# A two-step graph layer with guessed thresholds: gathers one by one, the laws' end later, two pieces of the end moved

## The chip, the cores and the metric

The kernel runs on one core of a Trainium2 chip. The engines are TensorE (PE, with PEld for its weight loads), VectorE (DVE), ScalarE (ACT), GpSimd (POOL) and SyncE (SP, which here only issues DMAs). Each engine takes its instructions in the order of its own queue, and waits for others through semaphores. The metric is the device time of one execution in microseconds (us), as a median of several runs; less is better. A profiled execution, a run of its own, gives the trace.

## What is computed

The inputs are x (3327 rows of 256) and an adjacency matrix adj (3327 x 3327, some 0.12% of it not zero, and its diagonal). The reference, cut to what matters:

```python
def _top_p_attention(X, W1, W2, W3):
    logits = (X @ W1.T @ W2.T) @ (X @ W3.T).T
    probs = softmax(logits, axis=-1)
    idx = argsort(-probs)
    sp = take_along_axis(probs, idx); cs = cumsum(sp)
    keep_sorted = cs - sp < 0.9            # the largest, up to a mass of 0.9
    A = probs * mask                       # mask: keep_sorted at its places
    return A / maximum(A.sum(-1), 1e-12)

h = maximum(_layernorm(x), 0.0)
R = (adj + eye) / row sums
Z, Xf, Xa = 0, h, h
for n in range(2):
    A = _top_p_attention(Xa, W1, W2, W3)
    Xf = R @ Xf
    Xa = A @ Xa
    Z = Z + Xf @ U1[n].T + Xa @ U2[n].T
out = x + layernorm(h + Z) * ln_g + ln_b
```

## The kernel before

The 3327 rows make 26 tiles of 128 (NT), the last of 127 rows. Both steps run over the tiles, as a pipeline that is written out by hand: in turn i of a step, tile i's threshold is settled, tile i + 1 is measured, tile i + 2 gets its logits, and the sums of tile i - 1 run on PE. The adjacency is so sparse that R @ X is done by gathering: for each row tile, and each of the 128 places within a column block, there is a list of the blocks that hold anything there; four of the list and one for what overflows are fetched by index, and the tile's own block is added (KT = 6).

For each tile and step:

- `weights` makes the exponentials e of one tile's logits (128 x 3328, PE and ACT).
- `measured` finds a threshold by guessing. `guessed` takes the row's sum Z and the row's "law" (mean, variance and what follows from them) to a first guess; then whole passes over e on ACT (L631, some 3.07 us each) count and sum what lies above. In the second step (`measured_twice`) there are three passes: two at the first guess, then one at a second guess that L682 to L686 compute; POOL makes small terms: L674 and L675 behind the first guess, L687 to L689 behind the second, L694 to L709 behind the third pass; ACT's L711 and DVE's L714 end it.
- `settle` on DVE: w (L728, e below the guess), 20 MAX8 over w (L733), six rounds of MAX8 and replace (L740, L742), the exact threshold (L747 to L752), and e masked by it in place (L762; in tiles 0 and 25 in two parts, L759, the first 1024 columns of 3328).
- `Sums` on PE: `turn` transposes four 128 x 128 blocks of e into PSUM (L811) and ACT copies them to SBUF (L813, eT); `sum` multiplies (L825) into one accumulator pa, of which there is one buffer. `turn` runs two groups ahead of `sum`. The transposes have two PSUM buffers.
- `gathered` (first step) and `refetch` (second step) fetch for R @ X: one DMA by SP for the adjacency blocks, and five gathers issued by POOL (L903, one instruction each) into xg, which has two buffers. `spread` multiplies them (L911) into one accumulator pr; DVE takes it out in L1086.
- `finish` in the second step, cut in pieces by `yield`: DVE takes the sum out of pa (L935), row statistics (L457, L458), POOL's L464, L465, L943, ACT's scaling (L950), POOL's L951 and L952, and the store.

`laws` makes the law of tiles 3 to 25 of the second step, after all of the first step is known. Eight pieces on PE and DVE (L556 to L562), then one end on POOL: a power of 0.5 (L567, a `pow` on 128 x 23) and nine small operations (L569 to L574). Tiles 0 to 2 have their own small laws.

The order is made by strings. Each turn has seven slots (PARTS); in a slot, each letter takes one piece of one generator: m and n are the measuring of tile i + 1 and of the turn before, d and c the settling, s `spread`, w and q the logits, g the gathers, l the laws, f `finish`. Between the slots PE's sums run. What is left of a generator at the end of a turn is run out in the order of a last string. PE, ACT and DVE then keep the order of the text; POOL keeps it from the second step on. A value is waited for where it is used, and everything behind that instruction on its engine waits too.

Before, one g issues all five gathers of a tile; turn -1 issues tile 0's in a slot and tile 1's at its end, behind the laws' end, and turn i issues those of tile i + 2. When all is done, `proof` tests whether every guess was good enough; if not, a slow search (`search_graph_layer`) computes all again.

Of the kernel before, what the change touches and what calls it, by code (L numbers as in the profile page):

```python
# [9 lines left out]
F32 = mybir.dt.float32  # L10
# [3 lines left out]
AF = mybir.ActivationFunctionType  # L14
ALU = mybir.AluOpType
# [3 lines left out]
P = 128  # L19
N = 3327  # L20
D = 256
DA = 64
NT = (N + P - 1) // P
# [297 lines left out]
LNY = 0.25 * math.log(0.72)  # L321

SQG, SQK = ((c[0], c[1] / (2 * c[0]), c[2] - c[1] ** 2 / (4 * c[0])) for c in (PG, PK))
# [15 lines left out]
KT = DIRECT + 2  # L339
# [5 lines left out]
def guess_graph_layer(ctx, tc, x, adj, w1t, w2t, w3t, u1t, u2t, ln_g, ln_b, out, flag):  # L345
    nc = tc.nc

    const = ctx.enter_context(tc.tile_pool(name="const", bufs=1))
    nodes = ctx.enter_context(tc.tile_pool(name="nodes", bufs=1))
    scan = ctx.enter_context(tc.tile_pool(name="scan", bufs=1))  # L350
    adjp = ctx.enter_context(tc.tile_pool(name="adjp", bufs=3))
# [9 lines left out]
    V, G, S, PE = nc.vector, nc.gpsimd, nc.scalar, nc.tensor  # L361

    rows_of = lambda t: min(P, N - t * P)
    valid = lambda t: 0 <= t < NT
# [41 lines left out]
    half = const.tile([P, 4], F32, tag="half", name="half")  # L406
    for k, c in enumerate((-0.5, 0.5, -1.0, -0.5)):
        G.memset(half[:, k : k + 1], c)
    halves = const.tile([P, NT], F32, tag="halves", name="halves")
    G.memset(halves, 0.5)  # L410
    law = const.tile([P, 7, NT], F32, tag="law", name="law")
    one = const.tile([P, 7], F32, tag="one", name="one")
    for k, c in enumerate((1.0, -1.0, 5.0e-4, SQG[1], SQK[1], math.log(10.0), LNY)):
        G.memset(one[:, k : k + 1], c)
    of_s = const.tile([P, 4], F32, tag="of_s", name="of_s")
    for k, c in enumerate((SQG[0], SQG[2], -SQK[0], -SQK[2])):
# [24 lines left out]
    bx = dram.tile([P, NT, D + 1], F32, tag="bx", name="bx")  # L441
    vx = dram.tile([P, NT, D], F32, tag="vx", name="vx")
# [4 lines left out]
    bb = const.tile([P, TOPK + 1], F32, tag="bb", name="bb")  # L447
# [100 lines left out]
    def laws(ts):  # L548

        at = lambda k, a, b: law[:, k, a:b]  # L550
        few_of = [ts[h::2][n : n + 3] for n in range(0, len(ts), 3) for h in range(2)]
        for few in filter(len, few_of):
            pq = ps_t.tile([P, 4, P], F32, tag="pt", name="pq")
            pm = pq.rearrange("p a b -> p (a b)")[:, : 3 * (2 * DA + 2)].rearrange("p (t n) -> p t n", t=3)
            for k, t in enumerate(few):
                PE.matmul(pm[:, k, :], query_of(t), qm[query_at(t), 1, :], start=True, stop=True)  # L556
            wide = scan.tile([P, NP], F32, tag="w", name="wide")
            mq = wide[:, : 3 * (2 * DA + 2)].rearrange("p (t n) -> p t n", t=3)
            V.tensor_copy(mq[:, : len(few)], pm[:, : len(few)])
            V.tensor_copy(law[:, 2, few[0] : few[-1] + 1 : 2], mq[:, : len(few), DA])  # L560
            for k, t in enumerate(few):
                V.scalar_tensor_tensor(mq[:, k, : DA + 1], mq[:, k, : DA + 1], 1.0, mq[:, k, DA + 1 :],  # L562
                                       ALU.mult, ALU.mult, accum_out=at(1, t, t + 1))
            yield
        a, b = ts[0], ts[-1] + 1
        s, var, m = (at(k, a, b) for k in range(3))
        G.tensor_tensor(s, var, halves[:, a:b], ALU.pow)  # L567
        for k, c in ((3, SQG[0]), (4, SQG[2]), (5, -SQK[0]), (6, -SQK[2])):
            G.tensor_scalar(at(k, a, b), s, c, 1.0e-4, ALU.mult, ALU.add)  # L569
        G.tensor_tensor(at(4, a, b), at(4, a, b), var, ALU.add)  # L570
        G.tensor_tensor(at(4, a, b), at(4, a, b), m, ALU.add)
        G.tensor_scalar(m, m, 0.25, LNY - 0.25 * math.log(0.1 / N), ALU.mult, ALU.add)
        G.tensor_scalar(var, var, 0.125, None, ALU.mult)
        G.tensor_tensor(var, var, m, ALU.add)  # L574
# [51 lines left out]
    def con(k):  # L626
        return one[:, k : k + 1]
# [247 lines left out]
    def gathered(t):  # L875
        oh = ohs.pop(t)
        ls, n = lists[:, t, :], LIST - DIRECT
        po = ps_t.tile([P, 4, P], F32, tag="pt", name="po")
        PE.matmul(po[:, 0, : n + 1], oh, ls[:, DIRECT:], start=True, stop=True)
        lo = small.tile([P, n], F32, tag="lo", name="lo", bufs=2)  # L880
        S.copy(lo, po[:, 0, :n])
        nth = small.tile([P, 1], F32, tag="nth", name="nth")
        S.activation(nth, po[:, 0, n : n + 1], AF.Identity, scale=-1.0, bias=part)
        yield
        of = small.tile([P, LIST], F32, tag="of", name="of", bufs=2)
        V.scalar_tensor_tensor(of[:, :n], place[:, :n], nth, lo, ALU.is_equal, ALU.mult, accum_out=nth)
        G.tensor_scalar(index[:, t, DIRECT:], nth, -1.0, float(NONE), ALU.mult, ALU.add)
        ac = adjp.tile([P, KT, P], F32, tag="ac", name="ac", bufs=2)
        nc.sync.dma_start(ac[:, KT - 1, :], adj[t, :, t, :])
        acs[t] = ac  # L890
        G.tensor_tensor(ac[:, KT - 1, :], ac[:, KT - 1, :], ident, ALU.add)
        rows = adj.rearrange("t p j r -> (t p j) r")
        for k in range(KT - 1):
            G.indirect_dma_start(out=ac[:, k, :], out_offset=None, in_=rows,  # L894
                                 in_offset=bass.IndirectOffsetOnAxis(ap=index[:, t, k : k + 1], axis=0),
                                 element_offset=t * P * NT * P)
        xgs[t] = fetched(bx, t, D + 1)

    def fetched(table, t, w):
        xg = adjp.tile([P, KT - 1, D + 1], F32, tag="xg", name="xg", bufs=2)  # L900
        rows = table.rearrange("p j d -> (p j) d")
        for k in range(KT - 1):
            G.indirect_dma_start(out=xg[:, k, :w], out_offset=None, in_=rows,  # L903
                                 in_offset=bass.IndirectOffsetOnAxis(ap=index[:, t, k : k + 1], axis=0))
        return xg


    def diffuse(ac, xg, own, w):
# [55 lines left out]
    live, ohs, acs, xgs, done, early = {}, {}, {}, {}, [], {}  # L964
    none = iter(())

    def run(work, n=99):
        for _ in range(n):
            next(work, None)
# [33 lines left out]
    for q in range(HALF + 5):  # L1003
        if 0 <= q - 3 < HALF:
            k, pk = q - 3, made.pop(q - 3)
# [17 lines left out]
        if 0 <= q - 2 < HALF:  # L1023
            k, pt = q - 2, turned.pop(q - 2)
# [10 lines left out]
        if 0 <= q - 1 < HALF:  # L1035
            k, rn = q - 1, scaled.pop(q - 1)
            pt = ps_t.tile([P, 4, P], F32, tag="pt", name="pt")
            for h in range(2):
                t = 2 * k + h
# [4 lines left out]
        if 0 <= q - 4 < HALF and 2 * (q - 4) in COUNTED:  # L1044
            k = q - 4
# [46 lines left out]
    def refetch(t):  # L1092
        acs[t] = adjp.tile([P, KT, P], F32, tag="ac", name="ac", bufs=2)
        nc.sync.dma_start(acs[t].rearrange("p k r -> p (k r)"), cx[t])
        xgs[t] = fetched(vx, t, D)
        yield

# [1 line left out]


    PLAN = (("mdsssa", "mcdsssa", "edawwp", "msda", "mpdea", "gdwwq", "emgq"),
            ("llcmss", "lnms", "lwwnfd", "lcmdsssg", "fmswqdf", "llmdf", "lmwfd"))

    LAST = {NT - 1: ("cfss", "cn", "ndd", "sss", "fddddsf", "f", "f"), NT: ("cf", "", "", "", "ff", "fv", "f"),
            NT + 1: ("fv", "f", "", "", "f", "f", "f")}
    LATE = (1, 4)
    trace, begin = nc.cur_bb.bb.instructions, len(nc.cur_bb.bb.instructions)
    work = dict(m=none, d=none, f=none)  # L1110
    later = {}
    ordered = []
    for step in range(2):
        sums = Sums(step, live, xw if step else x0, AHEAD[step])

        for i in range(-1, NT + 2):
# [4 lines left out]
            if step == 1 and i == -1:  # L1121
# [6 lines left out]
                c=work["d"],  # L1128
                d=settle(step, i, live[step, i]) if valid(i) else none,
                m=measured(step, live[step, i + 1]) if valid(i + 1) else none,  # L1130
                s=spread(step, i - 2 + 2 * step) if valid(i - 2 + 2 * step) else none,
# [1 line left out]
                e=first_end(i - 2) if step == 0 and valid(i - 2) else none,  # L1133
                a=itertools.islice(lister, 9 if i else 3) if step == 0 else none,
                p=packed(i + 1) if step == 0 and i >= 0 and valid(i + 1) else none,
                g=none if not valid(i + 2 * step) else refetch(i + 2) if step else gathered(i),
                b=none, q=none, v=proof() if step and i == NT else work.get("v", none),
                l=laws(range(3, NT)) if step and i == -1 else none,
            )
            if i >= 0 and valid(i + 3):  # L1140
                later[step, i + 3] = weights(step, i + 3, live)
# [9 lines left out]
                work["w"] = begun[2]  # L1151
            if step == 0 and i < 1:
                work["b"] = itertools.islice(product, MADE if i else NT)
            if step == 1 and i == -1:
                work["g"] = itertools.chain(refetch(0), refetch(1))
            for k in range(PARTS):
                g = PARTS * (i - 1) + k - LATE[step]
                summing = valid(g // PARTS)
                if summing and step:
                    sums.turn(g, min(i, NT - 1))  # L1160
                for c in "bb" + (LAST.get(i, PLAN[1]) if step else PLAN[0])[k]:
                    next(work[c], None)
                if summing and not step:
                    sums.turn(g, min(i, NT - 1))
                if summing:
                    ended = sums.sum(g)
                    if ended and step == 0:
                        live["r", ended[0]] = ended[1]
                    elif ended:
                        work["f"] = finish(ended[0], live.pop(("f", ended[0])), *ended[1])  # L1170
            if step == 1 and i == -1:
                run(work["m"])
            if step == 0 and i == -1:
                G.memset(es[2][:, N:NP], 0.0)
            for c in "lcnwqsepgb" if step else "cmwqsepgb":
                run(work[c])
            if step == 0 and i == NT:
                moments(1, gsum)
# [52 lines left out]
```

## Time and profile before

| | |
|---|---|
| three timed runs | 1426.26, 1431.23, 1432.77 us; median 1431.23 |
| profiled execution | 1383.37 us, its span 1381.4 us |
| busy: PE, DVE, ACT, POOL | 1271.7, 1207.6, 1109.1, 1022.8 us |
| first step ends, second begins | about 740 us |
| ACT pass L631 | 106 of 3.07 us |
| DVE L728 and L762, one | 3.83 and 3.84 us |
| POOL gather of the second step, L903 | 130 of 1.0 us |
| last operation on a tile ends, end of the trace | 1372.2 us, 1381.4 us |

The page lists groups of instructions by line; "out<-in" are the names of the program. The timeline lists instructions by start (us from the span's start), length, engine and line; in brackets stands how long the engine had been idle before, and what released it. In the windows the busy time of each engine in a stretch is given, with the number of its instructions.

### The profile page before, as it was taken

Reading aid. Unit: us, or ns where it says so; the run is one execution under the profiler, and the core shown is the slowest. Engines: PE = TensorE matmul, PEld = TensorE weight load, DVE = VectorE, ACT = ScalarE, POOL = GpSimd, SP = SyncE. Lnnn points to the kernel's source line nnn. Section 1 sums busy time; section 2 is a strip of 40 time slices with the busy share of each in tenths; the row PEclk is TensorE's granted clock in tenths of the full one; section 3 lists DMA queues with packets and bytes.
Section 4 is the critical chain, followed back from the end, with each engine's and each line's share of the span. In section 5 each row is a group of like instructions: output and inputs, shape, how many; then the busy total and the mean of one; then the engine's idle time right before and its main releaser. Section 6 shows DMA issues by size and latency. Waiting matters only on the chain.

```text
span 1381.4 us, 22149 instructions
## 1 busy us (share of the span) xinstructions
PE 1271.7 (92%) x6495; PEld 977.1 (71%) x6495; DVE 1207.6 (87%) x3595; ACT 1109.1 (80%) x2449; POOL 1022.8 (74%) x1374
## 2 busy tenths in 40 slices
PE   6898999999999999999997389999999999999885
PEld 5545777777877778787775267777776777777674
DVE  6878999999999999999944689999999999999992
ACT  5467888879888888888735689999999999999931
POOL 6225888888888888888843868888888888888832
PEclk9999999999999999999998589999999999999998
DMA  8884453545445453545331211212222221212100
GB/s 293 261 271 125 128 148 109 152 119 152 128 135 141 122 154 106 156 118 149 85 98 50 69 54 55 84 58 81 71 67 82 58 88 54 89 58 81 58 8 22
DMA packets 91202, 149.77 MB, mean 108 GB/s; under 512 B 15265, under 2 KB 58656, under 8 KB 91072
## 3 DMA queue, kind: packets, MB, share of 16 engines
q1 hardware_dynamic: 73616, 105.37, 24.4%
q0 software_dynamic: 16640, 42.69, 11.9%
q8 instruction: 54, 0.88, 0.3%
q14 instruction: 76, 0.62, 0.1%
q10 hardware_dynamic: 816, 0.20, 0.1%
HBM read 120.93 MB, written 27.28 MB: 107 GB/s over the span
## 4 chain that ended last, share of the span: by engine, by line
DVE 40%; PE 24%; ACT 17%; POOL 9%; DMA 4%; issue 4%; SPq 0%; POOLq 0%; DVEq 0%; ACTq 0%
ACT ja L631 11%; PE pa L825 9%; DVE e L762 9%; PE pl L598 5%; DVE cand L733 4%; DVE w L728 4%; DVE fm L847 4%; DVE bb L740 3%; DVE cand L742 3%; PE pt L811 3%; PE pz L988 3%; POOL xg L903 3%; POOL ac L894 2%; DVE x L762 2%; DMA at<-in_adj 2%
## 5 line engine op out<-in xcount | busy, mean ns | idle before, releaser
L825 PE MATMUL pa<-xw,eT 128*128 128x256 f32 x1352 | 330.8, 386 | 6.6 <-DVE s L935 6.5
L631 ACT ACTIVATE ja<-e,g 128x3328 uint8<-128x3328 f32 x106 | 325.8, 3074 | 0.1
L825 PE MATMUL pa<-x,eT 128*128 128x256 f32 x1352 | 323.1, 380 | 0.0
L825 PEld LDWEIGHTS pa<-xw,eT 128*128 128x128 f32 x1352 | 249.4, 191 | 67.9 <-issue 27.1
L825 PEld LDWEIGHTS pa<-x,eT 128*128 128x128 f32 x1352 | 243.7, 191 | 25.8
L733 DVE MAX8 cand<-w 128x8 f32<-128x168 f32 (+1 forms) x1040 | 251.5, 318 | 0.0
L813 ACT COPY eT<-pt 128x512 f32<-128x512 f32 (+1 forms) x364 | 201.9, 556 | 59.3 <-PE pt L811 58.8
L894 POOL DMA_INDIRECT ac<-in_adj,index x130 | 189.7, 1459 | 44.3 <-issue 30.5
L811 PE MATMUL pt<-ident,e 128*128 128x128 f32 x1144 | 180.1, 278 | 43.9 <-DVE e L762 21.9
L811 PEld LDWEIGHTS pt<-ident,e 128*128 128x128 f32 x1144 | 140.5, 144 | 90.2 <-issue 43.3
L903 POOL DMA_INDIRECT xg<-bx,index x130 | 158.0, 1216 | 39.2 <-issue 30.5
L728 DVE SCALAR_TENSOR_TENSOR w<-e,g 128x3328 f32<-128x3328 f32 x44 | 168.5, 3830 | 0.7
L903 POOL DMA_INDIRECT xg<-vx,index x130 | 130.9, 1007 | 45.6 <-issue 33.0
L762 DVE SCALAR_TENSOR_TENSOR e<-e,rec 128x3328 f32<-128x3328 f32 x40 | 153.6, 3840 | 0.6
L911 PE MATMUL pr<-xg,ac 128*128 128x257 f32 (+1 forms) x520 | 139.4, 392 | 11.3 <-DVE s L1086 11.1
L602 ACT ACTIVATE e<-pl 128x832 f32<-128x832 f32 x132 | 112.8, 859 | 30.2 <-PE pl L598 30.1
L911 PEld LDWEIGHTS pr<-xg,ac 128*128 128x128 f32 x520 | 94.0, 195 | 25.0 <-DVE s L1086 11.3
L740 DVE MAX8 bb<-cand 128x8 f32<-128x160 f32 x286 | 92.9, 325 | 6.4
L598 PE MATMUL pl<-after,qT 64*128 64x416 f32 x416 | 96.7, 559 | 0.6 <-ACT qT L527 0.6
L765 POOL TENSOR_TENSOR cum<-dr,bb 128x48 f32<-128x48 f32 x26 | 84.8, 3261 | 15.5 <-DVE rec L752 15.4
L951 POOL TENSOR_TENSOR s<-s,gam 128x256 f32<-128x256 f32 x25 | 92.6, 3703 | 3.2 <-ACT s L950 3.2
L598 PE MATMUL pl<-both,qT 64*128 64x416 f32 x416 | 90.1, 536 | 0.8 <-DVE both L1006 0.8
(257 smaller groups left out, 2200.0 us busy)
## 6 DMA issues: line engine op xcount, KB each, us to landing
at<-in_adj SPq DMA_DIRECT2D x102, 256.0 KB, 3.2
cx<-ac SPq DMA_DIRECT2D x26, 384.0 KB, 2.8
ac<-cx SPq DMA_DIRECT2D x26, 384.0 KB, 3.1
wide<-in_adj SPq DMA_DIRECT2D x10, 832.0 KB, 6.4
e<-in_adj SPq DMA_DIRECT2D x8, 832.0 KB, 5.1
bx<-e SPq DMA_DIRECT2D x26, 128.5 KB, 2.8
own<-bx SPq DMA_DIRECT2D x26, 128.5 KB, 3.2
x<-in_x SPq DMA_DIRECT2D x13, 256.0 KB, 5.4
```

The source lines that it names most:

```text
L598: PE.matmul(pl[:, a, :wd], qT[p, :], keys_of(step, a).rearrange("p a b -> p (a b)")[:, c : c + wd], start=True, stop=True)
L631: S.activation(ja, e, f, bias=guess, scale=sign, accum_out=total)
L728: V.scalar_tensor_tensor(w, e, col(16), e, ALU.is_lt, ALU.mult, accum_out=d2)
L733: V.max(cand[:, 8 * s : 8 * s + 8], w[:, s * SEG : min(NP, (s + 1) * SEG)])
L740: V.max(b8, cand)
L762: V.scalar_tensor_tensor(e, e, at(1), e, ALU.is_ge, ALU.mult, accum_out=ra)
L811: PE.transpose(pt[:, j, :], e[:, (j0 + j) * P : (j0 + j + 1) * P], ident)
L813: S.copy(eT[:, :w, :], pt[:, :w, :])
L825: PE.matmul(self.pa, eT[:, c - 4 * k, :], self.xa[:, j, :], start=c == 0, stop=c == NT - 1)
L894: G.indirect_dma_start(out=ac[:, k, :], out_offset=None, in_=rows, in_offset=bass.IndirectOffsetOnAxis(ap=index[:, t, k : k + 1], axis=0), ...
L903: G.indirect_dma_start(out=xg[:, k, :w], out_offset=None, in_=rows, in_offset=bass.IndirectOffsetOnAxis(ap=index[:, t, k : k + 1], axis=0))
L911: PE.matmul(pr[:, :w], ac[:, k, :], own if k == KT - 1 else xg[:, k, :w], start=k == 0, stop=k == KT - 1)
```

## The change

The five gathers of a tile become five pieces, and one generator `fetching` runs through all tiles in order. Strings for the first turns (OPEN) place them: in turn -1 five, one, and one at its end; in turn 0 three, one, and one at its end; in turns 1 to 3 five and one; from turn 4 on five in one slot as before. The laws' end moves from the end of turn -1 to the end of turn 0, and its power becomes Ln and Exp on ACT. In turn 25 (NT - 1), the `finish` piece that takes the third last sum (tile 23) out of pa stands before the twenty MAX8 and not between them, and in the turns 25 and 26 ACT's L950 of that tile stands some copies later.

```diff
-    halves = const.tile([P, NT], F32, tag="halves", name="halves")
-    G.memset(halves, 0.5)
-    one = const.tile([P, 7], F32, tag="one", name="one")
-    for k, c in enumerate((1.0, -1.0, 5.0e-4, SQG[1], SQK[1], math.log(10.0), LNY)):
+    one = const.tile([P, 8], F32, tag="one", name="one")
+    for k, c in enumerate((1.0, -1.0, 5.0e-4, SQG[1], SQK[1], math.log(10.0), LNY, 1.0e-12)):
...
-        G.tensor_tensor(s, var, halves[:, a:b], ALU.pow)
+        S.activation(s, var, AF.Ln, bias=con(7))
+        S.activation(s, s, AF.Exp, scale=0.5)
...
-        xgs[t] = fetched(bx, t, D + 1)
+        run(fetched(bx, t, D + 1))
 
     def fetched(table, t, w):
-        xg = adjp.tile([P, KT - 1, D + 1], F32, tag="xg", name="xg", bufs=2)
+        xgs[t] = xg = adjp.tile([P, KT - 1, D + 1], F32, tag="xg", name="xg", bufs=2)
         rows = table.rearrange("p j d -> (p j) d")
         for k in range(KT - 1):
             G.indirect_dma_start(out=xg[:, k, :w], out_offset=None, in_=rows,
                                  in_offset=bass.IndirectOffsetOnAxis(ap=index[:, t, k : k + 1], axis=0))
-        return xg
+            yield
...
-        xgs[t] = fetched(vx, t, D)
-        yield
+        yield from fetched(vx, t, D)
...
-            ("llcmss", "lnms", "lwwnfd", "lcmdsssg", "fmswqdf", "llmdf", "lmwfd"))
+            ("llcmss", "lnms", "lwwnfd", "lcmdsssggggg", "fmswqdf", "llmdf", "lmwfd"))
 
-    LAST = {NT - 1: ("cfss", "cn", "ndd", "sss", "fddddsf", "f", "f"), NT: ("cf", "", "", "", "ff", "fv", "f"),
+    LAST = {NT - 1: ("cfss", "cn", "nd", "sss", "fdddddsf", "f", ""), NT: ("c", "", "", "ff", "ff", "fv", "f"),
             NT + 1: ("fv", "f", "", "", "f", "f", "f")}
+    OPEN = {-1: ("llcmss", "lnms", "lwwnfd", "lcmdsssggggg", "fmgswqdf", "llmdf", "lmwfdm"),
+            0: ("cmssggg", "nms", "wwnfd", "cmdsss", "fmgswqdf", "mdf", "mwfd"),
+            1: ("cmss", "nms", "wwnfd", "cmdsssggggg", "fmswqdf", "mgdf", "mwfd")}
+    OPEN[2] = OPEN[3] = OPEN[1]
+    fetching = itertools.chain(*(refetch(t) for t in range(NT)))
...
-                g=none if not valid(i + 2 * step) else refetch(i + 2) if step else gathered(i),
+                g=fetching if step else gathered(i) if valid(i) else none,
...
-                l=laws(range(3, NT)) if step and i == -1 else none,
+                l=laws(range(3, NT)) if step and i == -1 else work["l"] if step and i == 0 else none,
...
-            if step == 1 and i == -1:
-                work["g"] = itertools.chain(refetch(0), refetch(1))
...
-                for c in "bb" + (LAST.get(i, PLAN[1]) if step else PLAN[0])[k]:
+                for c in "bb" + ({**OPEN, **LAST}.get(i, PLAN[1]) if step else PLAN[0])[k]:
...
-            for c in "lcnwqsepgb" if step else "cmwqsepgb":
+            if step and i < 1:
+                next(fetching)
+            for c in ("lcnwqsepb" if i > -1 else "cnwqsepb") if step else "cmwqsepgb":
```

## What I expected before the run

> **What bounds the kernel now.** I read the windows first, because two of the three edits touch single places and only a stage table shows what a place is worth. Columns: length, busy time of PE, PEld, DVE, ACT, POOL, the granted TensorE clock, DMA share, GB/s.
>
> ```profile
> 400.00:600.00 200.00, 198.84 (x1060) 158.02 (x1060) 190.56 (x579) 168.38 (x418) 164.35 (x193) 1.00 0.46 130
> ...
> 760.00:780.00 20.00, 8.10 (x22) 4.35 (x22) 12.61 (x40) 12.81 (x25) 15.92 (x27) 0.59 0.22 61
> 780.00:800.00 20.00, 7.30 (x28) 4.49 (x25) 14.89 (x40) 14.59 (x28) 17.12 (x21) 0.59 0.24 70
> ...
> 1000.00:1200.00 200.00, 188.81 (x969) 146.25 (x968) 185.31 (x520) 188.53 (x379) 170.38 (x225) 1.00 0.24 72
> ...
> 1340.00:1382.00 42.00, 24.93 (x132) 20.94 (x130) 13.80 (x42) 6.44 (x13) 9.72 (x17) 0.89 0.06 18
> ```
>
> The first step (to about 740 us) is PE's, 99% busy; the change hardly touches it. In the second step's steady part ACT, PE and DVE are all at 93 to 94%. Between them lies the opening, where PE works 8 of 20 us and POOL is the busiest, and after it the end, where PE works 25 of 42. There the waits are. The timeline of the opening gives the first pair: ACT waits for POOL, then DVE for POOL and ACT for DVE.
>
> ```profile
> 763.61 4.04 POOL L567 TENSOR_TENSOR law<-law,halves 128x23 f32<-128x23 f32 x1
> ...
> 771.00 1.12 POOL L903 DMA_INDIRECT xg<-vx,index  x1 [0.49 <-issue]
> ...
> 777.21 0.33 POOL L674 TENSOR_SCALAR g<-g,ms 128x1 f32<-128x1 f32 x1
> ...
> 777.57 0.29 ACT L685 ACTIVATE g<-g 128x1 f32<-128x1 f32 x1 [4.24 <-POOL g L674]
> ...
> 784.17 0.27 POOL L687 TENSOR_SCALAR g<-g 128x1 f32<-128x1 f32 x1
> 784.48 0.27 DVE L696 TENSOR_SCALAR g<-oa,g 128x1 f32<-128x1 f32 x1 [6.41 <-POOL g L687]
> ...
> 785.04 0.39 ACT L699 ACTIVATE g<-g,one 128x1 f32<-128x1 f32 x1 [3.63 <-DVE g L697]
> ```
>
> POOL is not slow at L674 and L687; they stand in its queue behind the end of the laws (763.61 to 770.51) and two bursts of five gathers (771.00 to 777.15, 778.12 to 784.13). The chain of waits confirms it: from 763.64 to 784.4 it runs on POOL almost alone. The timeline of the end gives the other pair.
>
> ```profile
> 1332.70 2.44 DVE L733 MAX8 cand<-w 128x8 f32<-128x168 f32 x10
> 1335.05 0.47 DVE L935 SCALAR_TENSOR_TENSOR s<-pa,ra,s 128x256 f32<-128x256 f32 x1
> ...
> 1335.58 3.44 PE L825 MATMUL pa<-xw,eT 128*128 128x256 f32 x8 [3.14 <-DVE s L935]
> ...
> 1349.45 0.60 ACT L950 ACTIVATE s<-s,nm,rstd 128x256 f32<-128x256 f32 x1 [7.16 <-POOL nm L943]
> 1349.96 0.84 ACT L813 COPY eT<-pt 128x512 f32<-128x512 f32 x2
> 1350.58 0.66 PE L811 MATMUL pt<-ident,e 128*128 128x128 f32 x4 [3.12 <-ACT eT L813]
> 1354.30 0.48 DVE L935 SCALAR_TENSOR_TENSOR s<-pa,ra,s 128x256 f32<-128x256 f32 x1 [5.70 <-PE pa L825]
> ```
>
> PE has one accumulator for the sums; it can't start tile 24 until DVE has read tile 23's out (L935), which stands behind ten MAX8. Later ACT sits 7.16 us in L950 while two finished transposes wait for their copies behind it.
>
> **What the Trainium skill says.** "SBUF — State Buffer", Who interferes with whom: a DVE instruction with two SBUF inputs contends with GpSimd instructions that read SBUF; the first to start holds the port for its whole length. The trace agrees: L709 takes 0.34 us in the median and 1.35 beside L759 (at 788.00), L765 takes 0.26 or 3.65, and a gather 0.95 or 4.54 beside L728. "TensorE: Matmul & The Clock Gate", Part 1: a PE that idles through a window falls to half rate. Here the windows show clock 0.59 in the opening and 0.68 in 1336 to 1340, just after the 3.14 us wait. "ScalarE: Activation LUTs", Table sets: Ln and Exp share a set, so the new pair needs no table load; L619 (Ln, 0.20 us) and L621 (Exp, 0.29 us) stand 0.6 us apart here, with no load between them.
>
> **The change, part by part.** Times are those of the trace before.
>
> *Gathers and laws, removed waits.* In the order of the two built programs POOL now has, after tile 0's five gathers and L687 to L689: one gather of tile 1, L694 to L709 of tile 0, one gather, L674 and L675 of tile 1, three gathers, L687 to L689, one gather of tile 2, L694 to L709, one gather, the laws' nine small operations, L765, L674, five gathers. The first lone gather goes into POOL's idle time 757.87 to 760.32. The second (pitch 0.95 + 0.30 = 1.25 us) starts at 763.9, and runs to 765 or, if held by DVE's L728, to 769 (from the 4.54 row). L674 then stands at 766.2 (it needs ACT's L673) to 769.3; ACT wants it at 773.4, so it no longer waits. L685 moves from 777.57 to 773.43, 4.1 us; tile 1's third pass ends at 777.3 instead of 781.4. The three gathers end by 773.8, L687 to L689 stand at 774.1 to 774.9, before they are wanted. What is late next is DVE: its MAX8 chain lasts to 778.07, so L696 runs at 778.1 and ACT's L699 at 778.65 instead of 785.04: 6.4 us.
>
> *The two ACT instructions* (square root as Ln and Exp, 128x23) stand on ACT behind L702 and are exposed: by the rows of L619 and L621 0.5 us with issue; bounds 0.4 to 0.8, by the 0.39 us rows. Their inputs (DVE's L562) were done at 759.7. Against it L711 no longer waits 0.78 us for L709: that was held by DVE's L759, and now L709 is through at 781.25, a quarter us before L759 starts (781.5). The pow of 4.04 us leaves POOL. So tile 2's first pass starts about 6.7 us earlier.
>
> *What POOL gives back.* Behind L709 stand now a gather, the laws (767.74 to 770.51, 2.8 us without the pow) and L765, and DVE has L759 at 781.5 to 785.3 and L728 at 786.2 to 789.9. If these hold POOL, the laws end at 792.6 and tile 2's L674 stands at 793.3; ACT wants it at 793.6. Just in time; 0 to 1 us, I take 0. Then five gathers and L687 to L689 last to 800.9, and the sixth gather to 802.15, where L694 could run at 801.55. So L709 comes 0.6 us late, after DVE's L762 has begun, and is held until that ends: ACT's L711 1.5 us late, of which the 0.61 us that ACT idles before the eT at 819.97 absorb a part: 0.9. In the next turn POOL idles 5.13 us before its gathers, and two of them no longer need that wait, so nothing is lost. In the turn of tile 3 the sixth gather meets 0.5 us of idle (before 852.08): again about 0.9. Together 1.8, bounds 0 and 2.6. From tile 4 on the order is that of before. The opening gains 6.7 - 1.8 = 4.9 us. PE's wait of 11.3 us for L1086 stays, since L1086 follows tile 1's second pass, which doesn't move. The laws' results are first wanted by tile 3's guess (L620 at 811.95), 12 us after they exist. DMA: all gathers of a tile stay issued before the turn that multiplies them; SP's order is unchanged.
>
> *Third last sum behind w.* L935 runs at 1332.7, right after L729; PE starts tile 24 at 1333.2, 2.4 us earlier. The 0.47 us only change places on DVE. PE then idles 0.8 us instead of 3.14, so I expect the first eight matmuls in 1.89 us (the row of every other group) and not 3.44: 3.9 us in all, and PE is at tile 25's first transposes at 1343.5. These need the first part of L759, done at 1344.59; PE started 0.15 us after it in the same case at 789.34. So they start at 1344.7.
>
> *ACT's end of it later.* L950 stands three copies later, so the copies at 1349.96 no longer wait and PE no longer for them: the transposes come at 1344.7 instead of 1350.58, 5.9 us. The sum of tile 24 ends 3.7 us on (1350.58 to 1354.28), at 1348.4; DVE is free at 1348.6 for its L935: 5.7 us earlier than 1354.30. After it PE runs 13.4 us without a pause to the end. L950 still waits for L943 at 1349.43, but only one copy (due 1348.7) stands behind it, and its sum comes at 1353: hidden. Bounds: 5.5 if the clock stays low, 2.4 if PE's other wait remains. I take 5.7.
>
> The other edits (a memset less, one column more) cost nothing: they lie under the first loads, before 6 us.
>
> Sum: 4.9 + 5.7 = 10.6 us of the profiled execution, 1383.37 us (span 1381.4 and 2.0 around it): 1372.8, 0.77%. The three timed runs were 43 to 49 us above it, so the profiled one was a quicker execution; I carry the ratio over: 1431.23 x 0.9923 = 1420.2, and say 1420.5.
>
> **Rivals.**
> - *The opening is given back.* POOL is at 17 of 20 us there, and the removed time is not work, only order. If L674 of tile 2 slips by 3 us (laws held twice by DVE) and both sixth gathers cost their upper bound, only the end's gain is left: 1425.5. Against it: ACT's two waits together are 7.9 us, and none of POOL's new places is more than 1 us late.
> - *The end gives only its first wait.* If tile 25's mask (L759) were needed whole, or ACT's queue stalled at another place, the end gains 2.4 us and the sum is 7.3: 1424. Against it the start at 789.34.
> - *Slower: POOL falls out of step.* Place: L709 of each turn. In the steady part POOL idles only 0.5 us before L694, and L709 ends 0.1 us before DVE's L762 starts. If the slip that I have in two turns stays in all, each of 22 more tiles pays 0.9 us, 20 us: 1440. It decides from twelve turns on. Against it: a turn that is held makes ACT 0.9 us later and so gives POOL that time back.
> - *It doesn't do what it says:* the rounding of Exp and Ln moves a guess, the proof fails and the search runs behind it: 27 rounds by 52 tiles by 3.07 us (the row of one pass), over 4 ms. The guesses are already made of such Ln and Exp.
>
> **How the numbers follow.** The forecast has 0.61, the opening given back 0.17, the end's half 0.12, POOL out of step 0.08, the failing proof 0.02. What a measurement here can tell from no change is 0.5%, 7.2 us: below 1424.1 is faster, above 1438.4 slower. Of the forecast nearly all is faster (0.57), of the two smaller gains half or a third (0.06 and 0.05): 0.68. Slower are the last two: 0.10. The rest, 0.22, is the same. The forecast's own range, by the bounds (opening 3.0 to 6.8, end 5.5 to 5.9) is 1418 to 1422; the three runs spread over 6.5 us, so 1412 to 1427. To leave out no more than two in ten it must reach the opening given back: 1412 to 1430.
>
> **What would show it.** Right: ACT's L685 and DVE's L696 without POOL waits in the opening; tile 2's first pass 5 to 7 us earlier; L935 at one place behind L729, the matmuls after it at 1.89 us a group; no 7 us wait at L950; the last L935 some 10 us earlier. Wrong: L674 as releaser of ACT in later turns, L709 over 1 us in many turns, or PE waiting for L813 or L759 at the end.

## The result and the profile after

| | before | changed |
|---|---|---|
| median, runs beside one another | 1429.2 us (7 runs) | 1416.46 us (7 runs) |
| range | 1426.26 to 1432.77 | 1414.25 to 1421.5 |
| ratio | | 0.9913, 95% interval 0.9894 to 0.9933 |
| profiled execution, its span | 1383.37, 1381.4 us | 1414.25, 1412.3 us |

The changed kernel is 12.4 us faster by the ratio (9.6 to 15.1 by the interval), though the two profiled executions say the opposite. They can't be compared as wholes: the first step runs in a quicker or a slower rhythm, or in a mixture of both, whatever the kernel (last section), and the profiled execution of the kernel before had the quicker one, so that its second step begins 41 us earlier (tile 0's first pass at 747.24, here at 788.59). So all places below are counted from tile 0's first pass of the second step. From there to the last L935, at the end of the last sum, it is 620.98 us before (1368.22 - 747.24) and 610.48 after (1399.07 - 788.59): 10.5 us less. Most lines after L409 stand one or two lower in the changed kernel: L935 became L934, L674 L673, L762 L761.

The first passes of tiles 0 and 2 in the kernel before:

```profile
747.24 3.05 ACT L631 ACTIVATE ja<-e,g 128x3328 uint8<-128x3328 f32 x1
...
789.59 3.06 ACT L631 ACTIVATE ja<-e,g 128x3328 uint8<-128x3328 f32 x1
```

The timeline of the opening after the change (start, length, engine, line; in brackets the idle time before, and what ended it):

```profile
788.59 3.05 ACT L630 ACTIVATE ja<-e,g 128x3328 uint8<-128x3328 f32 x1
...
810.62 3.07 ACT L630 ACTIVATE ja<-e,g 128x3328 uint8<-128x3328 f32 x1
814.79 0.29 ACT L684 ACTIVATE g<-g 128x1 f32<-128x1 f32 x1
...
819.90 0.39 ACT L698 ACTIVATE g<-g,one 128x1 f32<-128x1 f32 x1 [1.27 <-DVE g L696]
824.02 3.05 ACT L630 ACTIVATE ja<-e,g 128x3328 uint8<-128x3328 f32 x1
...
832.44 0.34 POOL L673 TENSOR_SCALAR g<-g,ms 128x1 f32<-128x1 f32 x1
...
835.91 0.29 ACT L684 ACTIVATE g<-g 128x1 f32<-128x1 f32 x1
```

L684 (before: L685, 4.24 us of waiting for POOL) has no bracket any more, and L698 waits 1.27 us for DVE and not 3.63. Tile 2's first pass stands at 824.02, 35.43 us from tile 0's; before it was 42.35. The last two lines are tile 2's: POOL's L673 is done 3.1 us before ACT's L684 needs it. The end, in the same view:

```profile
1369.35 0.47 DVE L934 SCALAR_TENSOR_TENSOR s<-pa,ra,s 128x256 f32<-128x256 f32 x1
1369.88 1.99 PE L824 MATMUL pa<-xw,eT 128*128 128x256 f32 x8 [0.80 <-DVE s L934]
...
1381.39 0.63 PE L810 MATMUL pt<-ident,e 128*128 128x128 f32 x4 [1.07 <-DVE e L758]
...
1386.09 0.60 ACT L949 ACTIVATE s<-s,nm,rstd 128x256 f32<-128x256 f32 x1 [1.23 <-DVE st L455]
...
1399.07 0.48 DVE L934 SCALAR_TENSOR_TENSOR s<-pa,ra,s 128x256 f32<-128x256 f32 x1 [6.32 <-PE pa L824]
```

PE waits 0.80 us instead of 3.14, its first eight matmuls take 1.99 us and not 3.44, and before tile 25's transposes it waits 1.07 us for DVE's mask and not 3.12 for ACT's copies. From the end of w (L729 at 1332.57 before, now L728 at 1369.22) to the last L934 it is 29.85 us, 35.65 before.

One place gives something back. In the turn of tile 3 POOL comes late by the sixth gather, DVE's mask of the tile begins at 890.02, and POOL's L707 runs as long as that does:

```profile
889.30 0.64 POOL L706 TENSOR_TENSOR g<-g,half 128x1 f32<-128x1 f32 x1
890.04 3.76 POOL L707 TENSOR_SCALAR g<-g 128x1 f32<-128x1 f32 x1
...
894.24 0.29 ACT L710 ACTIVATE g<-g 128x1 f32<-128x1 f32 x1 [1.29 <-POOL g L708]
```

The gain falls from 6.9 us (tiles 2 to 4) to 6.1 (tile 6 on), and is 5.9 us at tile 25's second pass. It is 4.7 at its third, and the next fence shows why:

```profile
1348.14 2.80 PE L824 MATMUL pa<-xw,eT 128*128 128x256 f32 x8 [2.49 <-DVE s L934]
...
1351.83 0.59 ACT L812 COPY eT<-pt 128x512 f32<-128x512 f32 x1 [2.24 <-PE pt L810]
```

The same group behind the same wait in the kernel before:

```profile
1312.73 1.99 PE L825 MATMUL pa<-xw,eT 128*128 128x256 f32 x8 [2.50 <-DVE s L935]
```

After an equal pause PE was at its low clock in one execution and not in the other; ACT's copy, and with it the pass, comes 1.2 us later. The windows of the changed kernel show that clock (the columns are those of the first table of the prediction, the granted clock third from the end):

```profile
1345.77:1349.18 3.41, 1.04 (x5) 0.94 (x6) 3.38 (x15) 2.03 (x5) 0.00 (x0) 1.00 0.00 0
1349.18:1352.59 3.41, 3.41 (x12) 2.77 (x11) 3.31 (x16) 1.14 (x4) 1.45 (x5) 0.50 0.00 0
```

The last section says what decides it. So the sum is 5.9 - 1.2 + 5.8 = 10.5, as found.

### The profile page after: what moved, and what is told of

It reads as the page before. It is cut to its first block, busy times and chain, and to the rows that moved or that the text cites. A ratio compares the mean times of both kernels' runs of the same rounds, so it can differ in the third digit from the quotient of the medians.

```text
span 1412.3 us, 22150 instructions
## 1 busy us (share of the span) xinstructions
PE 1280.5 (91%) x6495; PEld 975.2 (69%) x6495; DVE 1199.2 (85%) x3595; ACT 1108.5 (78%) x2451; POOL 957.0 (68%) x1373
## 4 chain that ended last, share of the span: by engine, by line
PE 50%; ACT 24%; DVE 18%; POOL 3%; issue 3%; DMA 0%; another core or an unknown queue 0%; ACTq 0%; DVEq 0%; POOLq 0%
PE pa L824 21%; ACT ja L630 12%; PE pt L810 8%; PE pl L597 6%; DVE e L761 5%; PE pr L910 4%; ACT eT L812 4%; PE pz L987 3%; PE pz L923 3%; DVE x L761 2%; DVE bb L739 2%; DVE cand L741 2%; DVE cand L732 2%; ACT e L601 1%; DVE w L727 1%
## 5 line engine op out<-in xcount | busy, mean ns | idle before, releaser
L810 PE MATMUL pt<-ident,e 128*128 128x128 f32 x1144 | 178.9, 276 | 35.5 <-DVE e L761 19.1
L893 POOL DMA_INDIRECT ac<-in_adj,index x130 | 130.4, 1003 | 44.5 <-issue 29.9
L761 DVE SCALAR_TENSOR_TENSOR e<-e,rec 128x3328 f32<-128x3328 f32 x40 | 153.2, 3829 | 0.6
L910 PE MATMUL pr<-xg,ac 128*128 128x257 f32 (+1 forms) x520 | 138.4, 391 | 10.5 <-DVE s L1085 10.5
L927 POOL TENSOR_TENSOR sv<-sv,x 128x256 f32<-128x256 f32 x26 | 20.7, 796 | 108.2 <-ACT sv L926 108.2
L764 POOL TENSOR_TENSOR cum<-dr,bb 128x48 f32<-128x48 f32 x26 | 79.2, 3046 | 15.5 <-DVE rec L751 15.3
```

What stands on the lines that cost most here:

```text
L761: V.scalar_tensor_tensor(e, e, at(1), e, ALU.is_ge, ALU.mult, accum_out=ra)
L810: PE.transpose(pt[:, j, :], e[:, (j0 + j) * P : (j0 + j + 1) * P], ident)
L910: PE.matmul(pr[:, :w], ac[:, k, :], own if k == KT - 1 else xg[:, k, :w], start=k == 0, stop=k == KT - 1)
```

## Experiments

All were read by the same places, in us from tile 0's first pass; "end" is from L729 (L728) to the last L935 (L934). Each row is one profiled execution; of e3, e4, e5 and e7 there is no other, so they have no ratio.

| kernel | tile 2, first pass | tile 10, first pass | tile 25, third pass | end | last L935 |
|---|---|---|---|---|---|
| before | 42.35 | 222.40 | 568.44 | 35.65 | 620.98 |
| changed | 35.43 | 216.34 | 563.72 | 29.85 | 610.48 |
| e1, end alone | 42.35 | 222.13 | 568.98 | 29.85 | 615.72 |
| e2, opening alone | 35.42 | 215.61 | 562.45 | 37.32 | 616.66 |
| e3, sum early | 42.38 | 223.51 | 569.61 | 38.55 | 625.07 |
| e4, scaling late | 42.32 | 221.87 | 568.73 | 30.88 | 616.49 |
| e5, gathers alone | 40.46 | 222.23 | 568.53 | 37.92 | 623.33 |
| e6, laws alone | 37.83 | 218.76 | 565.05 | 35.64 | 617.59 |
| e7, power on POOL | 35.04 | 216.61 | 564.31 | 30.45 | 611.65 |
| e8, extra gather earlier | 35.50 | 215.77 | 562.01 | 29.86 | 608.76 |
| e9, root in a gap | 34.97 | 215.97 | 563.42 | 30.44 | 610.74 |
| changed again | 35.44 | 216.03 | 563.03 | 29.84 | 609.76 |

### e1 and e2: are the two ends of the change independent?

e1 is the kernel before with the new line for turns 25 and 26, e2 the changed kernel with the old one:

```diff
-    LAST = {NT - 1: ("cfss", "cn", "ndd", "sss", "fddddsf", "f", "f"), NT: ("cf", "", "", "", "ff", "fv", "f"),
+    LAST = {NT - 1: ("cfss", "cn", "nd", "sss", "fdddddsf", "f", ""), NT: ("c", "", "", "ff", "ff", "fv", "f"),
```

> The kernel before with the strings of turns 25 and 26 alone changed. Read from the end of tile 25's w (L729) to the last L935: 35.65 us in the kernel before, 29.85 in the changed one. My theory, that the end is a chain of its own (PE's wait for L935, then for the copies behind L950): 29.9 us, so 5.8 less, and the time 5.8 us (0.4%) below the kernel before, ratio 0.996. Rival, only the first wait is removed and the rest of the end in the changed kernel came from the opening: 33.2 us, ratio 0.998.

> The changed kernel with the old strings in turns 25 and 26: the opening's edits alone. My theory: tile 2's first pass 6.9 us nearer to tile 0's first than in the kernel before (35.4 us, not 42.35), 6.0 us nearer from tile 6 on after the turn with the sixth gather gives 0.8 back, and the end from L729 to the last L935 takes 35.6 us as in the kernel before; ratio 0.996. Rival, the two ends hang together (a later phase of POOL at the end): the end is not 35.6 but over 1 us away from it.

e1's ratio is 0.9953 (0.9937 to 0.9970), 6.7 us, and its end takes 29.85 us, as my theory had it; the first wait alone would leave 33.2. e2's ratio is 0.9965 (0.9948 to 0.9983), 5.0 us. Its tile 2 stands 6.9 us nearer, tile 10 6.8, more than the 6.0 expected. Its end is 37.32 us and not 35.6, which was the mark of the rival. But it isn't a matter of POOL: PE's first group there took 1.99 us, and the low clock came instead behind the second wait (4.56 us long), where a group took 3.24. The two ratios add up to 6.7 + 5.0 = 11.7 of the 12.4 us, within their intervals what the changed kernel gains.

### e3 and e4: the end's two edits

e3 is the kernel before with only the sum earlier, e4 with only ACT's L950 later:

```diff
-    LAST = {NT - 1: ("cfss", "cn", "ndd", "sss", "fddddsf", "f", "f"), NT: ("cf", "", "", "", "ff", "fv", "f"),
+    LAST = {NT - 1: ("cfss", "cn", "nd", "sss", "fdddddsf", "f", "f"), NT: ("cf", "", "", "", "ff", "fv", "f"),
...
-    LAST = {NT - 1: ("cfss", "cn", "ndd", "sss", "fddddsf", "f", "f"), NT: ("cf", "", "", "", "ff", "fv", "f"),
+    LAST = {NT - 1: ("cfss", "cn", "ndd", "sss", "fddddsf", "f", ""), NT: ("c", "", "", "ff", "ff", "fv", "f"),
```

> The kernel before, with only the third last sum's L935 taken out behind w, ACT's L950 at its old place. My theory, a chain in which ACT's L950 still waits for L943 and holds both finished transposes: PE starts tile 24 some 2.4 us earlier, but its transposes of tile 25 come when they came before; from L729 to the last L935 35.6 us, gain 0 (within 0.5). Rival, the two edits add up: 3.9 us of the 5.8 come from this one, 31.8 us.

> The kernel before, with only ACT's L950 (and what follows it) later, L935 at its old place between the MAX8. My theory: PE's first wait of 3.1 us for L935 stays, its second of 3.12 us for the copies goes; from L729 to the last L935 35.65 - 3.1 = 32.5 us. With the other run this makes 0 + 3.1, not 5.8: the parts need each other. Rival, they add up: 5.8 - 3.9 = 1.9 us, 33.7 us.

e3's timeline of the end:

```profile
1379.77 1.99 PE L825 MATMUL pa<-xw,eT 128*128 128x256 f32 x8 [0.80 <-DVE s L935]
...
1395.98 0.60 ACT L950 ACTIVATE s<-s,nm,rstd 128x256 f32<-128x256 f32 x1 [10.94 <-POOL nm L943]
...
1397.10 1.12 PE L811 MATMUL pt<-ident,e 128*128 128x128 f32 x4 [6.89 <-ACT eT L813]
1398.01 3.62 PE L825 MATMUL pa<-xw,eT 128*128 128x256 f32 x8
```

PE's first wait is gone, as planned, and the time has moved whole into the second: 6.89 us for the copies behind L950, which waits 10.94 us where it waited 7.16. Tile 25's transposes stand 17.99 us from L729, and stood 18.01 in the kernel before: gain 0 there, as I had said. The trace shows why: L943, for which L950 waits, needs DVE's L457, and this stands in DVE's queue behind the whole mask L759, 14.87 us behind L729 here and 14.88 before, however early the sum is taken out. After the long pause PE is at its low clock (3.62 us for a group of 1.89), and the end is 2.9 us longer than in the execution of the kernel before, but only 0.6 us longer than in e5, which has the old end. Moved alone, the sum gains nothing; that it costs something is not shown by one execution. In e4 the first wait stays and the second goes:

```profile
1383.20 1.99 PE L825 MATMUL pa<-xw,eT 128*128 128x256 f32 x8 [3.14 <-DVE s L935]
...
1393.47 0.60 PE L811 MATMUL pt<-ident,e 128*128 128x128 f32 x4
...
1397.07 0.60 ACT L950 ACTIVATE s<-s,nm,rstd 128x256 f32<-128x256 f32 x1 [0.15 <-POOL nm L943]
```

The transposes follow with no wait, 13.28 us from L729. The gain is 4.8 us: the 3.1 I had expected and 1.6 more, since after the 3.14 us pause PE's group took 1.99 us in this execution and 3.44 in that of the kernel before. Neither theory's figure holds for e4, but the additive one (0 or less, and 4.8, for 5.8) is out: the earlier sum is worth 1.0 us with the late L950 (more where PE's first group behind the pause falls into its low clock), and nothing without it.

### e5 and e6: which work on POOL stood in the way?

e5 has the gathers one by one, the laws' end as it was. e6 has the laws' end later (with Ln and Exp), the gathers in bursts. Both keep the old end of the kernel. Against the changed kernel, e5:

```diff
-        S.activation(s, var, AF.Ln, bias=con(7))
-        S.activation(s, s, AF.Exp, scale=0.5)
+        G.tensor_tensor(s, var, halves[:, a:b], ALU.pow)
...
-                l=laws(range(3, NT)) if step and i == -1 else work["l"] if step and i == 0 else none,
+                l=laws(range(3, NT)) if step and i == -1 else none,
...
-            for c in ("lcnwqsepb" if i > -1 else "cnwqsepb") if step else "cmwqsepgb":
+            for c in "lcnwqsepb" if step else "cmwqsepgb":
```

and e6 against the kernel before (and the Ln and Exp of the change):

```diff
+    LAST = {0: ("cmss", "nms", "wwnfd", "cmdsssg", "fmswqdf", "mdf", "mwfd"),
...
-                l=laws(range(3, NT)) if step and i == -1 else none,
+                l=laws(range(3, NT)) if step and i == -1 else work["l"] if step and i == 0 else none,
...
-            for c in "lcnwqsepgb" if step else "cmwqsepgb":
+            for c in ("lcnwqsepgb" if i > -1 else "cnwqsepgb") if step else "cmwqsepgb":
```

> The kernel before with the gathers one by one, the laws' end left in turn -1 with its power on POOL (the end of the kernel is that of the kernel before). Read from tile 0's first pass to tile 2's first: 42.35 us before, 35.43 in the changed kernel. First theory, that POOL's queue needs to lose only one of the two pieces of work that stood in front of L674 and L687: about 5.5 us less, 36.9 (35.4 to 38.5). Rival, each piece has its own share of the 6.9 and the two add up: about 3.5 us less, 38.9.

> The kernel before with the laws' end moved to the end of turn 0, with Ln and Exp on ACT, and the gathers in bursts as they were. First theory (only one of the two pieces has to go): about 6 us less to tile 2's first pass, 36.4 us (35.4 to 39), and nothing lost in the turn of tile 3, since no sixth gather stands there: tiles 6 to 24 some 6 us nearer, as in the changed kernel. Rival (shares that add up): 3.5 us less, 38.9, and together with the other run 6.9.

The first theory fails in e5. In e6 the 37.83 us lie in its range (35.4 to 39), but tile 6 stands 3.7 us nearer and not 6. e5 gains 1.9 us at tile 2, and what is left of it at tile 10, 0.2, is less than executions with one and the same order differ there (below). Its timeline:

```profile
767.86 1.10 POOL L903 DMA_INDIRECT xg<-vx,index  x1 [0.17 <-issue]
768.37 3.69 DVE L728 SCALAR_TENSOR_TENSOR w<-e,g 128x3328 f32<-128x3328 f32 x1
768.99 6.97 POOL L567 TENSOR_TENSOR law<-law,halves 128x23 f32<-128x23 f32 x1
...
779.08 0.30 ACT L685 ACTIVATE g<-g 128x1 f32<-128x1 f32 x1 [1.68 <-POOL g L674]
...
787.06 1.28 DVE L759 SCALAR_TENSOR_TENSOR e<-e,rec 128x1024 f32<-128x1024 f32 x1
787.21 1.58 POOL L707 TENSOR_TENSOR g<-g,half 128x1 f32<-128x1 f32 x1
788.89 2.18 POOL L708 TENSOR_SCALAR g<-g 128x1 f32<-128x1 f32 x1
...
791.51 0.30 ACT L711 ACTIVATE g<-g 128x1 f32<-128x1 f32 x1 [3.74 <-POOL g L709]
```

One gather ahead of the power puts the power's start behind that of DVE's L728, and it takes 6.97 us, 2.9 more than the 4.04 in which it ran before DVE began. ACT then waits 1.68 us for L674, the third pass comes 1.6 us later than in the changed kernel, and so POOL's L707 and L708 fall into DVE's mask L759 and take 3.8 us instead of 0.9; ACT waits 3.74 us more. A lateness of 1.6 us has become 5.0. In e6 it is the second gather of the burst that DVE's L728 holds (3.40 us), and the ten gathers stand before L686 (784.55), so that ACT's L698, which follows it over DVE, waits 3.20 us, two more than in the changed kernel. e6 gains 4.5 us at tile 2, 3.6 at tile 10; ratio 0.9961 (0.9945 to 0.9977). The two gains make 6.4 of the 6.9, nearer to the rival, though not its even shares. What each piece costs is less its own length than which DVE pass the piece behind it meets.

### e7: was POOL's time at the new place full?

```diff
-        S.activation(s, var, AF.Ln, bias=con(7))
-        S.activation(s, s, AF.Exp, scale=0.5)
+        G.tensor_tensor(s, var, halves[:, a:b], ALU.pow)
```

> The changed kernel with the laws' power back on POOL, at the new place. What I said of the place: tile 2's L674 is just in time, so that POOL has nothing to spare there. Then the power (4.0 us before) makes it 1.3 to 4 us late, as far as it isn't hidden in the time in which DVE holds POOL anyway, and tile 2's third pass starts 0.8 to 3.5 us later than in the changed kernel (50.71 us from tile 0's first pass: 51.5 to 54.2), since ACT loses two instructions of 0.5 us. Rival, POOL has slack: it comes 0.5 us earlier, at 50.2.

Tile 2's first pass comes 0.39 us earlier, which is the price of the two ACT instructions. Its third is at 50.85, 0.14 us later than in the changed kernel, below my range. The laws' last operation came 1.5 us later and not 4, since DVE held POOL there in any case. DVE then waited 2.52 us for POOL's L765 and ACT 3.19 us for DVE, but most of that lies beside a wait that ACT has without it too: in the turn's copy before the third pass it waits for PE (1.34 us in e8), which was at its low clock until shortly before (0.50 from 795 to 799 us in e8). So POOL was not as full as "just in time" says. At tile 10 e7 is 0.3 and 0.6 us behind the two executions of the changed kernel, which is less than executions with one order differ, so the square root's move to ACT is worth little, if anything.

### e8, e9 and the changed kernel again

e8 has one gather more in turn 0, where POOL waits for ACT, and none in the slot of turn 3. e9 is e8 with the law's Ln and Exp before tile 1's third pass:

```diff
-            0: ("cmssggg", "nms", "wwnfd", "cmdsss", "fmgswqdf", "mdf", "mwfd"),
+            0: ("cmssggg", "nms", "wwnfd", "cmdsss", "fmggswqdf", "mdf", "mwfd"),
...
-    OPEN[2] = OPEN[3] = OPEN[1]
+    OPEN[2] = OPEN[1]
```

```diff
         S.activation(s, s, AF.Exp, scale=0.5)
+        yield
...
-            0: ("cmssggg", "nms", "wwnfd", "cmdsss", "fmggswqdf", "mdf", "mwfd"),
+            0: ("cmssggg", "nms", "wwnfd", "cmdsss", "fmggswqdf", "lmdf", "mwfd"),
```

> The changed kernel with one gather more in turn 0, where POOL stood 1.34 us idle before L693, and none in the slot of turn 3 where L707 was held by DVE for 3.76 us. My theory, that the sixth gather of that turn gave back the 0.8 us: tile 5's first pass 0.8 to 1.4 us nearer than in the changed kernel (105.85 us from tile 0's first: 104.4), tile 10's 0.7 us nearer, nothing lost in turn 0; time 0.7 us below, not to be seen in the ratio (0.991). Rival, the hold moves on to another turn or turn 0 pays the 1.25 us: tile 10 at its place in the changed kernel (216.34) or later.

> The kernel with the extra gather earlier, and the laws' Ln and Exp on ACT placed before tile 1's third pass, so that they fall into the 1.27 us that ACT waits afterwards for DVE's MAX8 chain. My theory, that the two were exposed for 0.4 us: tile 2's first pass at 35.1 us from tile 0's first (35.50 without this), and what follows 0.4 us nearer up to the end; time 0.4 us less, not to be seen in a ratio. Rival, ACT is not what limits there: no pass after tile 2's second moves.

> The changed kernel once more, beside its successor and the kernel before on one chip. Theory, that 1.2 us at tile 25's third pass were a low PE clock of that one execution and not the change: the step from its second pass to its third is 7.5 us, or 8.4 to 8.7 again with PE's matmuls behind the 2.5 us wait at 2.8 us a group and not 1.99; from tile 0's first pass to tile 10's 216.3 us again, and 29.9 us at the end; ratio 0.991. Rival, the step is always 8.7 us with this order: then the change costs 1.2 us there.

In e8 L707 takes 0.34 us in the turn of tile 3 and L710 waits for nothing; tile 5's first pass is at 104.60 (105.85 in the changed kernel, 105.54 in its second run), tile 10's 0.6 and 0.3 us nearer than in those. With the sixth gather the mask holds L707 (3.76 us) in the changed kernel's first execution, and the next instruction, L708, in its second and in e2 (3.59 and 3.58 us). So the sixth gather was the cause of the hold. What is left of it at tile 10 is less than executions differ: e2, which has it, stands at 215.61 there. Ratio to the kernel before 0.9901 (0.9883 to 0.9919). e9's tile 2 comes 0.5 us earlier, as expected, but its third pass later (51.17 to 50.79), with a PE group of 3.69 us where e8 had 2.77: at tile 10 nothing is left, and the rival stands. Its ratio, 0.9874 (0.9837 to 0.9910), can't be told from the 0.9900 (0.9866 to 0.9935) of the changed kernel beside it. e8's last L935 is the earliest of all, 1.0 us before the better run of the changed kernel, too little for a ratio to show.

The changed kernel's second execution takes 8.41 us between tile 25's second and third pass, with groups of 2.47 and 2.72 us, so it is again at the low clock there. That alone could be the change's doing. But e1, with the opening of the kernel before, took 8.36, e4 8.35, and e8, with nearly the order of the changed kernel, 7.52: it isn't the order.

## Why the prediction was right

It said 1420.5 us (range 1412 to 1430), ratio 0.9923; 1416.46 and 0.9913 were measured. That the places give 10.5 us beside the 10.6 said is in part luck: the opening gave 5.9 us and not 4.9, and a low clock that the change didn't cause took 1.2 back. By its steps:

- *Gathers and laws*: 6.7 us for tile 2's first pass; 6.9 measured, in four executions with the full opening 35.4 to 35.5 us. The order of what is late next was right too: DVE's MAX8 chain ends ACT's wait at L698. What I didn't see is what each part gives alone (1.9 us in e5, 4.5 in e6): in the prediction their removal was one sum.
- *The two ACT instructions*: 0.5 us said, 0.39 by e7.
- *What POOL gives back*: 1.8 us said, 0.9 of it in turn 1 and 0.9 in the turn of tile 3. The second came (0.8 us, L707 held by DVE's mask), the first didn't: there L693 still waited 1.22 us for ACT, since tile 2's third pass came later than I had it, and L708 was through at 845.93, 0.1 us before the mask. This term was too large by one turn.
- *L674 of tile 2*: it was said to be just in time. Nothing was lost, but it was done 3.1 us before ACT came to L684 (832.44 and 835.91), since ACT was later there than I had it; so even e7's power fitted in.
- *End*: 5.7 us said, 5.8 measured, in e1 as well, and at the place I had named (DVE's first part of the mask, then DVE). My 3.9 us for the earlier sum alone is right for PE's start and for nothing else: e3 shows it to be worth nothing without the later L950. The likely reading of a profile, that each removed wait is worth its length, fails here: the sum of the two was right because I followed the chain to its next limit.
- *Slow clock*: I booked 1.5 us for PE's faster first group as a certain gain. It isn't one: in the executions with the old end the low clock came after the first pause or after the second. After the first it cost nothing, since with L950 at its old place tile 25's transposes stand 18.0 us behind L729 in all five executions, whether PE's first group took 3.44 or 1.99 us. After the second it did: the old end took 35.6 to 37.9 us, the new one 29.8 to 30.5. So the end is worth 5.2 to 8.1 us by the pair of executions compared, which may be part of why the measured 12.4 lies above my 10.6. The first step may be another part: in the changed kernel's profile it ended 4 to 6 us earlier than in e1 to e4 (tile 0's first pass at 788.59, and at 792.59 to 794.58). No run separates the two.
- *Port*: in the part on the Trainium skill I took it that the first of DVE and POOL to start holds the other off for its whole length. The runs show this where DVE starts first. Where POOL's power started first (763.61 in the kernel before, 789.57 in e7), DVE's pass beside it wasn't longer than elsewhere (L728 at 764.32 took 3.69 us, the second part of L759 at 789.65 took 2.62). None of the sums rested on that half.
- *Rivals*: the opening given back and the end's half are out by e2 and e1. POOL out of step for all turns didn't come: the held turn cost 0.8 us once, and L707 took 0.35 us in the next turns. One later turn has such a hold (L707 at 1068.87, 3.60 us), and the kernel before has it too (L708 at 1033.43, 3.70 us). The guesses held: no execution shows a search behind the second step.

## What to carry to other kernels

When one engine waits twice in a chain, undo each wait alone before you price it: an edit that only moves the idle time to the next wait is worth nothing, and may cost something if the longer pause lowers PE's clock. Book such a change of the clock as a range, not as a certain gain. On POOL ask of every moved instruction which long DVE pass it now starts beside, and of every lateness which pass the instructions behind it will then meet. Where executions differ more than the edit is worth, count from a fixed event near the place and not from the start of the span.

## What the runs showed of the hardware

- A pause of PE of 2.5 to 7 us is followed by a group of eight matmuls in anything from 1.99 to 3.69 us, with the same order and the same pause: 1.99 and 2.80 after 2.5 us, 1.99 and 3.44 after 3.14 us. The traces' records of the granted clock show what decides it. In each of the twelve traces every stretch at half the clock begins and ends on a grid of 3.41 us intervals, and the grid lies otherwise to the kernel in each execution. What counts is how much of the pause falls into one interval: of the 2.5 us, 2.37 in the changed kernel (from 1345.77 to 1349.18; the next interval has clock 0.50), but 1.0 and 1.5 us in two intervals in the kernel before; of the 3.14 us, 2.69 in one interval in the kernel before, but 1.2 and 1.9 in two in e2. Between tile 25's second pass and the last sum, over all twelve traces, fifteen intervals with 1.97 us or more without a matmul were followed by one at half the clock; one with 2.02 (e8) and all with 1.93 or less were not. So a pause needn't fill a whole window, though the prediction speaks of one, but this bound is that of one place: in the first step of the layer 1.65 us were enough in three traces (492.4 us in the changed kernel).
- Four executions with the opening of the kernel before have tile 10 at 221.87, 222.13, 222.40 and 223.51 us. Whether the clock explains this too I haven't shown.
- POOL's power on 128 x 23 takes 4.0 us (4.04 and 4.07) and 6.97 when DVE's L728 had begun 0.6 us before it; in e7 it began 0.08 us before a part of DVE's mask and took 4.07.
- The first step has two rhythms, one with about 24 us a turn and one with about 26. In a turn of e1 (the kernel before had a median of 1428.13 us beside it), POOL's timeline shows

```profile
397.97 0.73 POOL L928 TENSOR_TENSOR sv<-sv,x 128x256 f32<-128x256 f32 x1 [4.44 <-ACT sv L927]
...
401.94 3.14 POOL L540 TENSOR_TENSOR ms<-ms,half 128x1 f32<-128x1 f32 x1
```

and in the profiled execution of the kernel before, whose POOL order in the first step is the same,

```profile
376.72 0.73 POOL L928 TENSOR_TENSOR sv<-sv,x 128x256 f32<-128x256 f32 x1
...
383.38 0.59 POOL L540 TENSOR_TENSOR ms<-ms,half 128x1 f32<-128x1 f32 x1
```

In the first, POOL waits for ACT, its power then falls beside a long DVE pass, and PE is busy 95% of the time from 400 to 600 us and not 99%; the second step begins 47 us later (tile 0's first pass at 794.20). In another set of runs, that of e5 to e8, the kernel before had a median of 1389 us (12 runs), and the four profiles of that set have the quicker rhythm (750 to 754). In the third set, that of e9 and the changed kernel again, the median of the kernel before was 1418 us (13 runs), and the two profiles have a mixture of both (777 and 770). This is what the rival "POOL out of step" would have been, in another place. What starts it was not tried.
